# Issuing the load of the filter's rows from GpSimd's queue in a spectral convolution

## The chip, the cores and the metric

The kernel runs on one core of one Trainium2 chip. The metric is device time in microseconds of one execution; the time before is the median of three runs. One more execution was taken by the hardware profiler, and every duration below comes from that one. Engines are named as in the profile: PE is TensorE (PEld its weight loads), DVE is VectorE, ACT is ScalarE, POOL is GpSimd, SP is SyncE; SPq and POOLq are the queues in which an engine's sequencer takes its instructions, DMA issues among them.

## The reference

The input `x` is four images of 512 x 512 pixels with 16 channels, float32. There are two residual layers, each on a group-normalised input (8 groups). Layer 0 is a long convolution: a 16 x 16 matrix of transfer functions is made from 8 x 8 polynomial coefficients, `x` is transformed on a zero-padded 1024 x 1024 grid, each frequency is multiplied with the 16 x 16 matrix, and the result is transformed back and cut. Layer 1 is a 3 x 3 convolution with a normalisation, an arccos and two tanh factors.

```
X = jnp.fft.rfft2(x, s=(2 * l1, 2 * l2), axes=(-3, -2))
Y = jnp.einsum('...hwi,ijhw->...hwj', X, H_full)
y = jnp.fft.irfft2(Y, s=(2 * l1, 2 * l2), axes=(-3, -2))
```

## The kernel before

Four stages follow one another. `filter_phase` builds the filter's spectrum and leaves it in device memory as `g_d`. `forward_phase` transforms the normalised images along one axis and leaves them as `x_d`. `conv_phase` takes one row of the spectrum after another, does the transform along the other axis, the product and the way back, and stores `y_d`. `last_phase` finishes the inverse transform and does layer 1. The change is in `conv_phase` alone.

`conv_phase` works through 513 rows (`rows`, line 719; the first two are two halves of one row and take the `plane` branch). For each row there are these pieces:

- `load_x(n)` (line 743) brings the row of the images, 256 KB, into one of two buffers `x`.
- `load_g(n)` (line 731) brings the row of the filter, 128 partitions of 8 KB, 1024 KB in all, into one of two buffers `g`.
- `x_part(n, b)` (line 769) multiplies `x` with a DFT matrix on PE into `px`, which ACT and DVE copy to `xe`.
- `x_late(n)` (line 784) runs on POOL: it stores `xe` to `xf_d` (448 KB), makes a turned copy `xl` with four multiplications, a multiplication and an addition (lines 798 to 800), and stores `xl` to `xf_d` too (448 KB). Then `half_shift` copies two halves within the chip on ACT.
- `load_xe(n)` (line 812) reads `xf_d` back at shifted offsets, with two DMAs of 1536 KB each. These are the shifted copies. They read what both stores of `x_late(n)` wrote, so they wait until those have landed.
- `g_part(n, j)` (line 821) multiplies `g` with a DFT matrix on PE into `pg`, which is copied to `gh`. The last of them, j = 15, frees the buffer `g`.
- `mix(n, g)` (line 838) multiplies `gh` with `xe` on PE. It needs the shifted copies.
- `over_q` (line 858) and `over_g` (line 888) turn the product back on PE, DVE, ACT and POOL (`zd` and `z`, lines 882 and 884), and store `yo` to `y_d` from POOL (line 914, 256 KB).

`step(n)` (line 922) is a software pipeline: in it row n is mixed, row n + 1 has its filter transformed and its shifted copies loaded, row n + 2 has its images transformed, turned and stored, row n + 2 has its filter loaded, row n + 3 has its images loaded, and rows n - 1 and n - 2 are turned back. So `mix(n + 1)` comes two steps after `x_part(n + 1)`.

An automatic scheduler (Tile) sets the order of instructions within each engine's queue, from the data dependencies, the buffers and its own estimate of when each instruction can start; it also sets the waits. A queue is worked in order: an instruction that waits holds all behind it. In the trace the SP queue has, in each row, the order first half of the shifted copies, filter row, second half of the shifted copies, image row. The POOL queue has `xu`, store of `xe`, `xu`, `xl`, store of `xl`, store of `yo`, `zd`, `z`.

Of the kernel before, what the change touches and what calls it, by code (L numbers as in the profile page):

```python
# [46 lines left out]
P = 128  # L47
# [148 lines left out]
def dram(t, row, offset, *dims):  # L196

    pitch = t.shape[1]
    lead = [[pitch, t.shape[0]]] if row is None else []
    return bass.AP(tensor=t.tensor, offset=t.offset + (row or 0) * pitch + offset,  # L200
                   ap=lead + [list(d) for d in dims])
# [494 lines left out]
def conv_phase(tc, cst, g_d, x_d, y_d):  # L696
    nc = tc.nc
    with ExitStack() as ctx:
# [32 lines left out]
        def load_g(n):  # L731
            rc, r, plane = rows[n]
            g = io.tile([P, C, 8 * C], F32, name="g")
            t, w = g.rearrange("p j x -> p (j x)"), C * 8 * C
            if plane is None:
                nc.sync.dma_start(out=t, in_=dram(g_d[rc], r, 0, [w, P], [1, w]))
            else:
                for to, at in ((0, (0, 96)[plane]), (64, (64, 32)[plane])):
                    nc.sync.dma_start(out=t[to : to + 32], in_=dram(g_d[rc], r, at * w, [w, 32], [1, w]))
                    nc.gpsimd.memset(t[to + 32 : to + 64], 0.0)  # L740
            state["g", n] = g
# [180 lines left out]
        def step(n):  # L922
# [7 lines left out]
            if row(2):  # L930
                load_g(n + 2)
# [505 lines left out]
```

## Time and profile before

| what | value |
|---|---|
| median of 3 runs | 16687.61 us (16677.77 to 16700.49) |
| the profiled execution | 16676.9 us |
| its span | 16675.0 us |
| mean granted PE clock | 0.97 |
| first and last `g_part` matmul (about the length of `conv_phase`) | 4762.5 to 13817.4 us |
| busy PE / DVE / ACT / POOL over the span | 90% / 64% / 54% / 62% |
| device memory traffic over the span | 270 GB/s |
| DMA share, 6000 to 13700 us | 0.87 at 322 GB/s |

Busy time says how long an engine worked, not what it waited for; the ends of matmuls are modelled, and a busy PE is not a PE at its peak. A wait is read as "who waited, for whom, how long in total, how often, the longest". For a DMA the row of the issue shows only the issuing; its bytes move later, on 16 DMA engines that all queues share. The DMA share of a stretch is the mean busy share of those 16 engines; it can pass 1 slightly, since packets overlap.

### The profile page before, as it was taken

The numbers are of one execution on the slowest core, as the hardware profiler recorded it, in microseconds if no ns is written. First come the engines' busy times: TensorE is split into PE (matmuls) and PEld (weight loads), VectorE is DVE, ScalarE is ACT, GpSimd is POOL, SyncE is SP. The second block draws the span as 40 slices with busy tenths as digits, with TensorE's granted clock in tenths as the row PEclk, the third lists the DMA queues.
The fourth block names the chain that finished last, engine by engine and source line by source line (L and its number), as shares of the span: only waits on it lengthen the run. The fifth ranks groups of instructions, "written<-read, shape, count | busy, mean of one in ns | idle before, by whom it ended". The sixth has DMA issues, their size and how long they took to land. (4 is left out here: it accounts for less than half of the span.)

```text
span 16675.0 us, 545650 instructions
## 1 busy us (share of the span) xinstructions
PE 15084.4 (90%) x232588; PEld 11256.3 (68%) x232588; DVE 10610.7 (64%) x22299; ACT 9049.8 (54%) x18799; POOL 10372.0 (62%) x10669
## 2 busy tenths in 40 slices
PE   7999999998988898888888898888888888988888
PEld 5555555554557777777777777777777777867777
DVE  8999999993545555555555555555555552357877
ACT  5666666663345555555555555555555551027888
POOL 7777777772346666666666666666666660237766
PEclk7999999999999999999999999999999999989999
DMA  4888788878878888888888888888888886885531
GB/s 134 231 237 236 233 241 234 237 227 259 248 267 323 325 326 317 321 320 318 321 324 324 325 325 321 324 324 321 324 321 321 324 322 230 312 291 164 169 108 70
DMA packets 2914698, 4543.40 MB, mean 272 GB/s; under 512 B 126114, under 2 KB 2094460, under 8 KB 2801422
## 3 DMA queue, kind: packets, MB, share of 16 engines
q1 hardware_dynamic: 2703070, 3836.37, 67.4%
q0 software_dynamic: 172336, 605.00, 9.4%
q10 hardware_dynamic: 36864, 67.13, 1.2%
q8 instruction: 1833, 30.03, 0.7%
q14 instruction: 595, 4.87, 0.1%
HBM read 3030.71 MB, written 1477.31 MB: 270 GB/s over the span
## 5 line engine op out<-in xcount | busy, mean ns | idle before, releaser
L829 PE MATMUL pg<-c_dg,g 64*128 64x128 f32 x32832 | 2837.4, 290 | 357.0 <-ACT gh L729 186.6
L845 PE MATMUL pm<-xe,gh 128*32 128x64 f32 x131328 | 2386.6, 222 | 538.5 <-issue 286.2
L845 PEld LDWEIGHTS pm<-xe,gh 128*32 128x32 f32 x131328 | 2007.6, 110 | 1133.5 <-issue 933.1
L829 PEld LDWEIGHTS pg<-c_dg,g 64*128 64x128 f32 x32832 | 2286.2, 190 | 692.3 <-issue 260.3
L874 DVE TENSOR_TENSOR z<-zq,pz 128x256 f32<-128x256 f32 x2052 | 861.6, 420 | 2667.5 <-ACT zq L873 2597.6
L727 DVE COPY gh<-pg 128x512 f32<-128x512 f32 x2046 | 1409.9, 689 | 1242.8 <-PE pg L829 1237.6
L449 PE MATMUL pt<-ev_in,c_todd 128*128 128x512 f32 x4096 | 1928.0, 609 | 108.6 <-ACT u L337 83.4
L798 POOL TENSOR_TENSOR xu<-xe,c_late 128x256 f32<-128x256 f32 x2052 | 1394.3, 705 | 863.7 <-ACT xe L729 842.8
L506 DVE RECIPROCAL dn<-dn 128x256 f32<-128x256 f32 x1024 | 1718.1, 1718 | 0.0
L729 ACT COPY yf<-pm 128x512 f32<-128x512 f32 x2046 | 1211.0, 592 | 915.4 <-PE pm L845 901.4
L381 POOL TENSOR_TENSOR sp<-m,dn 128x512 f32<-128x512 f32 x1024 | 1302.6, 1273 | 611.8 <-DVE dn L506 527.1
L809 ACT COPY xe<-xl 64x1024 f32<-64x1024 f32 x513 | 538.7, 1050 | 1895.8 <-POOL xl L800 1895.8
L449 PEld LDWEIGHTS pt<-ev_in,c_todd 128*128 128x128 f32 x4096 | 728.6, 190 | 1022.1 <-issue 701.5
L729 ACT COPY gh<-pg 128x512 f32<-128x512 f32 x2058 | 1201.2, 584 | 378.9 <-PE pg L829 376.6
L866 PE MATMUL pz<-c_ident,yf 128*128 128x128 f32 x8208 | 1372.2, 290 | 29.9 <-issue 17.3
L397 PEld LDWEIGHTS pg<-c_dinv,sp 64*128 64x128 f32 x16384 | 1004.2, 196 | 466.2 <-ACT sp L386 211.4
L408 ACT COPY st<-pg 128x256 f32<-128x256 f32 x2048 | 617.6, 391 | 1281.9 <-PE pg L397 1281.9
L800 POOL TENSOR_TENSOR xl<-xl,xu 128x1024 f32<-128x1024 f32 x513 | 1209.7, 2358 | 40.2
L397 PE MATMUL pg<-c_dinv,sp 64*128 64x128 f32 x16384 | 1106.6, 287 | 72.4 <-ACT sp L386 48.3
L882 POOL TENSOR_TENSOR zd<-z 128x512 f32<-128x512 f32 x513 | 653.1, 1273 | 771.7 <-DVE z L874 771.7
L914 POOL DMA_DIRECT2D y_d<-yo x511 | 297.3, 582 | 1332.6 <-ACT yo L729 1306.8
L1280 PE MATMUL pc<-l_band,xn 128*128 128x160 f32 (+2 forms) x6144 | 1072.9, 333 | 52.2 <-DVE e_o L1335 51.9
(211 smaller groups left out, 30943.8 us busy)
## 6 DMA issues: line engine op xcount, KB each, us to landing
xe<-xf_d SPq DMA_DIRECT2D x1026, 1536.0 KB
g<-g_d SPq DMA_DIRECT2D x511, 1024.0 KB
g_d<-st SPq DMA_DIRECT2D x256, 1024.0 KB
ev_in<-g_d SPq DMA_DIRECT2D x1024, 256.0 KB
g_d<-ot SPq DMA_DIRECT2D x1024, 256.0 KB
xf_d<-xe POOLq DMA_DIRECT2D x513, 448.0 KB, 8.3
xf_d<-xl POOLq DMA_DIRECT2D x513, 448.0 KB, 5.5
x_d<-xo SPq DMA_DIRECT2D x128, 1024.0 KB
```

What stands on the lines that cost most here:

```text
L381: nc.gpsimd.tensor_mul(w["sp"], w["m"], bc(w["dn"], 2, [P, 2, 2, P]))
L397: nc.tensor.matmul(pg[u][:, n, k].rearrange("p a x -> p (a x)"), w["sp"][q, k, c, :], dinv[q, 2 * kp + k, c, :], start=(c == 0), stop=(c = ...
L449: nc.tensor.matmul(pt, todd[:, c, kc, hh * P : hh * P + P], ev[:, kc, c], start=(kc == 0), stop=(kc == 1),)
L506: nc.vector.reciprocal(w["dn"], w["dn"])
L727: nc.vector.tensor_copy(dst, src)
L729: nc.scalar.copy(dst, src)
L798: nc.gpsimd.tensor_mul(u[:, :, h, c], xe[:, :, h, 1 - c], bc(late[:, 1 + c], 2, [P, F, 2]))
L800: nc.gpsimd.tensor_add(xl.rearrange("p f h c k -> p (f h c k)"), xl.rearrange("p f h c k -> p (f h c k)"), u.rearrange("p f h c k -> p (f ...
L829: nc.tensor.matmul(pg[c][:, j % 4], g[half, j], dg[half], start=True, stop=True)
L845: nc.tensor.matmul(pm[32 * q : 32 * q + 32, g % 8], gh[:, f].rearrange("p c j -> p (c j)"), xe[:, :, f].rearrange("p t h c k -> p t (h c k ...
L866: nc.tensor.transpose(pz[:, t % 4].rearrange("p v q x -> p (v q x)"), y[:, at].rearrange("p g x -> p (g x)"), ident)
L1280: nc.tensor.matmul(pc[:, lo:hi, :].rearrange("p w j -> p (w j)"), xns[q][:, h * P + dh : h * P + dh + P], bands[dh][:, o : o + hi - lo, :] ...
```

## The change

The load of a whole filter row is issued by POOL and no longer by SP. The four half loads of the first two rows stay in SP's queue. Source, destination, buffers and size of the transfer are the same.

```
         def load_g(n):
             rc, r, plane = rows[n]
             g = io.tile([P, C, 8 * C], F32, name="g")
             t, w = g.rearrange("p j x -> p (j x)"), C * 8 * C
             if plane is None:
-                nc.sync.dma_start(out=t, in_=dram(g_d[rc], r, 0, [w, P], [1, w]))
+                nc.gpsimd.dma_start(out=t, in_=dram(g_d[rc], r, 0, [w, P], [1, w]))
             else:
```

More of the change, by code (lines that the diff above doesn't have):

```diff
@@ L735, in load_g @@
             if plane is None:
-                nc.sync.dma_start(out=t, in_=dram(g_d[rc], r, 0, [w, P], [1, w]))
+                nc.gpsimd.dma_start(out=t, in_=dram(g_d[rc], r, 0, [w, P], [1, w]))
             else:
```

## The prediction

> **What bounds the kernel now.** I read the page first for the stages, then the waits of PE and SP in the row loop, then the order of time of one row on SP and POOL, and then the DMA share microsecond by microsecond.
>
> The page, its PE row and the slices of DMA:
>
> ```profile
> span 16675.0 us, 545650 instructions
> PE 15084.4 (90%) x232588; PEld 11256.3 (68%) x232588; DVE 10610.7 (64%) x22299; ACT 9049.8 (54%) x18799; POOL 10372.0 (62%) x10669
> DMA  4888788878878888888888888888888886885531
> ```
>
> No engine is full, and neither is DMA. In the row loop, which lasts from about 4750 to 13850 us, PE waits for these (us in total, times, longest):
>
> ```profile
> PE pm L845 <- issue: 286.2, 305, 3.2
> PE pg L829 <- ACT gh L729: 186.6, 204, 3.9
> PE pg L829 <- issue: 167.3, 100, 3.4
> PE pm L845 <- DMA xe<-xf_d: 110.7, 75, 3.5
> ```
>
> The fourth line is what the change can reach: 110.7 us in which `mix` stood for the shifted copies, in 75 of some 511 rows, 1.5 us each. Four more rows of that answer name DVE instructions that `mix` doesn't read (z L878 14.8, zq L875 12.2, z L874 10.1, pz L876 8.0; 45.1 us together); part of these may be the same wait under another name. SP's own waits in the same stretch:
>
> ```profile
> SPq L815 <- DMA xf_d<-xl: 6612.7, 512, 15.5
> ...
> SPq L736 <- PE pg L829: 113.5, 140, 11.4
> SPq L736 <- PE pz L866: 92.1, 104, 1.8
> ```
>
> SP stands 12.9 us in every row (6612.7 / 512) until the store of `xl` has landed. Only then does it issue the shifted copies, and the filter row comes behind the first of them. One row in order of time, SP and then POOL:
>
> ```profile
> 9025.13 0.37 SPq L815 DMA_DIRECT2D xe<-xf_d  x1
> 9025.62 0.41 SPq L736 DMA_DIRECT2D g<-g_d  x1
> 9026.07 0.43 SPq L815 DMA_DIRECT2D xe<-xf_d  x1
> ```
>
> ```profile
> 9020.86 0.58 POOL L791 DMA_DIRECT2D xf_d<-xl  x1 [0.29 <-POOL xl L800]
> 9023.82 0.58 POOL L914 DMA_DIRECT2D y_d<-yo  x1 [2.37 <-ACT yo L729]
> 9026.38 1.27 POOL L882 TENSOR_TENSOR zd<-z 128x512 f32<-128x512 f32 x1 [1.98 <-DVE z L874]
> 9027.73 1.27 POOL L884 TENSOR_TENSOR z<-z 128x512 f32<-128x512 f32 x1
> 9030.07 1.36 POOL L798 TENSOR_TENSOR xu<-xe,c_late 128x256 f32<-128x256 f32 x2 [1.07 <-ACT xe L729]
> ```
>
> And the same stretch in windows of 1 us (after the colon: length, busy of PE, PEld, DVE, ACT, POOL, clock, DMA share, GB/s):
>
> ```profile
> 9023.00:9024.00 1.00, 1.00 (x58) 0.91 (x48) 0.87 (x3) 0.75 (x3) 0.18 (x1) 1.00 0.72 240
> 9024.00:9025.00 1.00, 1.00 (x18) 0.88 (x15) 0.79 (x4) 0.49 (x2) 0.40 (x1) 1.00 0.17 70
> 9025.00:9026.00 1.00, 1.00 (x26) 0.71 (x27) 0.65 (x2) 0.83 (x2) 0.00 (x0) 1.00 0.63 238
> 9026.00:9027.00 1.00, 1.00 (x64) 0.91 (x54) 0.90 (x4) 0.10 (x1) 0.62 (x1) 1.00 0.72 111
> 9027.00:9028.00 1.00, 1.00 (x15) 0.88 (x14) 0.72 (x3) 0.53 (x2) 0.92 (x2) 1.00 0.98 365
> ```
>
> There is a hole in the DMA traffic of each row, while SP waits for `xl` and until the first bytes of the shifted copies move; before and after it the engines are full. The trace also has a record of each DMA packet. Averaged over 380 rows and placed by the issue of the first shifted load (time 0), the DMA share is 0.97 at +14, 0.73 at +15, then 0.55, 0.26, 0.16 for the three microseconds about the next issue, 0.79 and then full from +2 on. That is a hole of some 2.5 us a row.
>
> The loop behind it runs over two rows. From the start of a `mix` to `x_part` is 2.6 us (9008.46 to 11.07), from there to the issue of the `xl` store 9.8 us (to 9020.86), to its landing and the first shifted load 5.7 us (landing 5.5 in the median), from there to the last packet of the shifted copies 15.1 us (median of the packet records), and about 1.2 us until the landing is known (estimate: the fastest `xl` store lands 3.4 us after issue, of which 2.2 are 1.13 to its first packet and 1.1 of packets). Sum 34.4 us for two steps, 17.2 us a row. PE alone needs 16.9: a third of the rows take 16.89 to 16.96 us from `x_part` to `x_part`, and these don't wait for the shifted copies. The mean row takes 17.6 us (513 rows from 4758.1 to 13785.4). So the loop and PE are nearly level; PE gains on the loop in quiet rows, catches up, and waits. The rest over 16.9 is PE's own ("issue" 1.0 us a row, and reduced clock now and then) and isn't touched.
>
> **What the skill says.** "DMA: Bandwidth & Descriptors", section Issuing engines are not separate DMA queues: DMAs from any engine run on the same 16 DMA engines, and another issuer saves only issue time. The packet records agree as to rate: 4 KB packets take 159 ns in POOL's queue and in SP's. The same page, section Queues, rings and completion order: each DMA engine takes turns between queues, a packet at a time, and within a queue works in ring order. The trace agrees in part: at +10 both queues move (0.34 and 0.66 of the engines). So `g` in SP's ring stands between the two shifted loads; in POOL's it stands behind the stores of `xl` and `yo` and shares with SP's. The same page, Specifications: first byte after about 1 us from GpSimd, about 0.6 us from Sync. Here it is 1.13 us after a `yo` store and 1.03 us after a shifted load, but 4.4 us after the `xe` store, which has POOL's multiplications behind it.
>
> **The change, part by part.**
>
> *SP loses one issue a row*, 0.44 us in the median, and with it the wait for `g_part` ahead of it: (113.5 + 92.1 + 15.4 + 7.5) / 511 = 0.45 us a row. The second shifted load is issued up to 0.9 us earlier. Worth nothing by itself: its bytes stand behind the first one's, 24 packets of 159 ns = 3.8 us on each engine.
>
> *POOL gains one issue a row.* The nearest row is the `yo` store, also 128 partitions, 0.58 us; 511 x 0.58 = 298 us of POOL time. It must wait for the last `g_part` of row n, which ends 2.1 us before the first shifted load in the median (4.0 us before `x_part` starts). I place it where it becomes free: after the `yo` store, ahead of `zd`. POOL idles there (1.98 us in the row shown; 771.7 us over 509 rows), because `zd` needs results that PE makes after that `g_part`. So it costs 0; behind it stand `zd`, `z` and the whole of `x_late`, so without the cover it would be 0.58 us a row in the two-row loop, 0.29 a step, up to 150 us; below zero it cannot go.
>
> *The bytes move earlier.* `g` is 8 packets of 309 ns on each engine, 2.5 us. Issued at -2.0 with 1.13 us to the first packet it starts at -0.9, behind what is left of the stores; the shifted load's packets start at +1.03. Of those 1.9 us about 1.5 are free (share 0.16 to 0.26 taken). So about 1.5 us of the 2.5 are moved in the hole, and the rest shares with the first shifted load. The last packet of the shifted copies comes 1.5 us earlier, at 13.6 instead of 15.1. Bounds: 0 (`g` starts no earlier than now) and 2.5 (all in the hole, in rows where PE is ahead and `g_part` ends at -3 or before). The loop becomes (34.4 - 1.5) / 2 = 16.45 us, below PE's 16.9: what is late next is PE itself.
>
> *The sum.* Of 110.7 us, with 1.5 us of relief against waits of 1.5 us mean and a loop with slack, I take 85% away: 94. Of the 45.1 us under other names a third: 15. Against this some 20 us for PE's waits named "issue": if they are instruction fetches over the same DMA engines, then filling the hole takes from them what the emptier end of the row gives back; bounded by 50 us either way, a tenth of their 521 us. Net -89 on the profiled execution, 16676.9 to about 16588; the median stood 11 us above that, so 16600. In POOL's queue `g` is needed 15.5 us after its present issue (shortest tenth about 14), and it lands within 11 now, earlier then: no new wait on PE.
>
> **The rivals.**
>
> *Hidden anyway (0.17), about 16680.* The shifted copies wait for bytes, and the bytes are the same. If POOL reaches the load only when the first shifted load goes out too, both queues share and the last packet stays at 15.1. For: in a quarter of the rows `g_part` ends less than 1 us before that issue. Against: those are the rows in which PE is behind and doesn't wait.
>
> *Slower (0.14), about 16950.* The load stands behind `zd` and `z` in POOL's queue, issued at +3.9 in the row shown. Then its packets, starting at +5 to +8, lie in one ring ahead of the `xe` store (issued at +5.3), and the `xl` store behind both lands up to 2.5 us later. The loop grows to (34.4 + 2.5) / 2 = 18.45; against today's 17.6 that is at most 0.8 us, over 511 rows 430 us, and half of it where they overlap less, with 260 as its value. It decides as soon as `xl` lands over 0.5 us later than now. For: the queue of POOL is in order, and the scheduler may put the load late. Against: `g_part` ends before the last `over_q`, which `zd` needs, so the load is ready first.
>
> *Larger gain (0.07), about 16480.* The `xl` store, its contention gone too, lands 1 us earlier, and PE's "issue" waits shrink by a fifth with the shorter backlog. Speaks against it: the total of bytes a row is unchanged.
>
> The forecast has 0.62.
>
> **How the numbers follow.** This kernel's measurement can tell about 0.2% from no change, 33 us, so 16654 and 16721 are the limits. Faster: 0.62 + 0.07 = 0.69. Same: 0.17. Slower: 0.14. The likeliest's own range is 16540 to 16650 (the hold of the 110.7 us and the bounds of the issue term). The range runs from 16510, which leaves out most of the larger gain, to 16730, which takes in no change and the edge of the slower case.
>
> **What would show it.** Right: in POOL's order the load of `g` between the `yo` store and `zd`, issued before the first shifted load; the DMA share in the hole risen; PE's wait for the shifted copies under 30 us; PE's "issue" near 521 us; rows of 16.9 us in more than half of the row loop. Wrong: the load behind `z`; the landing of `xl` above its 5.5 us or of `xe` above 8.3; `zd` or `xu` waiting for POOL's issue; or a new wait of `g_part` for `g`.

## The result

The changed kernel takes 16789.28 us in the median of four runs (16773.5 to 16796.37). On the same chip the kernel before took 16682.69 (16665.89 to 16700.49). The ratio is 1.0062 with the interval [1.0045, 1.0080]: slower by about 107 us. The prediction said 16600 and faster.

**The profile after.** The head of the page, its PE row, its DMA slices, and the table of DMA queues (packets, MB, share of 16 engines' time):

```profile
span 16771.7 us, 545635 instructions
PE 15112.5 (90%) x232588; PEld 11245.3 (67%) x232588; DVE 10630.4 (63%) x22299; ACT 9107.3 (54%) x18799; POOL 10634.8 (63%) x11180
...
DMA  4788887888878888888888888888888886885531
...
q1 hardware_dynamic: 2629486, 3300.51, 58.1%
q0 software_dynamic: 245920, 1140.85, 18.9%
q10 hardware_dynamic: 36864, 67.13, 1.2%
q8 instruction: 1833, 30.03, 0.7%
```

The span is 96.7 us longer, and PE works 28 us of that (15112 against 15084); the rest it waits. All of it lies in the row loop: from the first `x_part` to the last it was 9027.3 us before and is 9124.8 now. The row loop before and after (length; busy of PE, PEld, DVE, ACT, POOL; clock, DMA share, GB/s):

```profile
4758.10:13785.40 9027.30, 8062.22 (x183716) 6454.86 (x183717) 4900.70 (x13245) 4759.39 (x8679) 5763.23 (x5624) 0.98 0.87 322
4754.80:13879.60 9124.80, 8087.89 (x183717) 6440.42 (x183718) 4922.02 (x13245) 4817.45 (x8679) 6029.63 (x6134) 0.98 0.87 319
```

PE worked 26 us longer in the loop and stood 72 us longer (965 before, 1037 after). The filter's bytes went from q1 to q0. The last line of the queue table becomes important below: a queue named "instruction", 0.7% of the engines, the same 1833 packets in both kernels.

PE's waits in the row loop (total us, times, longest), the answer to the four lines shown of before:

```profile
PE pm L845 <- issue: 630.0, 559, 4.3
PE pg L829 <- issue: 170.0, 127, 3.7
PE pm L845 <- ACT zq L873: 80.8, 224, 0.7
PE pg L829 <- ACT gh L729: 57.8, 71, 4.1
...
PE pm L845 <- DMA xe<-xf_d: 0.2, 1, 0.2
```

The wait that the change was to take away went from 110.7 to 0.2 us, and the wait for ACT's copies of `gh` from 186.6 to 57.8. In their place stands "issue", the profile's name for time in which an engine waits for nothing that it shows: `mix` 630.0 instead of 286.2, `g_part` 170.0 instead of 167.3, and with the three smaller groups 896 us instead of 521. All of PE's waits in the loop, whatever they are named, add up to 980 us before and 1047 after: of the 375 us that "issue" gained, 307 are taken from other waits.

One row on POOL and then on SP:

```profile
9025.53 0.58 POOL L914 DMA_DIRECT2D y_d<-yo  x1 [3.34 <-ACT yo L729]
9027.06 0.54 POOL L736 DMA_DIRECT2D g<-g_d  x1 [0.94 <-PE pg L829]
9028.31 1.27 POOL L882 TENSOR_TENSOR zd<-z 128x512 f32<-128x512 f32 x1 [0.71 <-DVE z L874]
9029.67 1.26 POOL L884 TENSOR_TENSOR z<-z 128x512 f32<-128x512 f32 x1
```

```profile
9026.30 1.79 SPq L815 DMA_DIRECT2D xe<-xf_d  x2
9032.19 0.33 SPq L748 DMA_DIRECT2D x<-x_d  x1
```

The load of `g` stands where the prediction put it, between the store of `yo` and `zd`, in time in which POOL idled. In this row it goes out 0.8 us behind the first shifted load; in two rows of three it goes out ahead of it. The landing of the `xl` store (min, median, max), before and then after:

```profile
DMA to landing us min/median/max: 3.4/5.5/8.7
```

```profile
DMA to landing us min/median/max: 3.4/4.2/10.0
```

It lands 1.3 us earlier, so the shifted loads start earlier too. The filter, the `xl` store and the shifted copies all came earlier, and PE lost more than that won.

**What "issue" is here.** The waits called "issue" sit at fixed places. I counted all that PE's sequencer takes, in its order: matmuls, weight loads and the instructions on semaphores between them. Of the matmuls' "issue" gaps over 0.4 us in the row loop, 377 of 378 before and 650 of 651 after come at the same place of each group of 256 instructions. The trace has 2 x 232588 matmuls and weight loads and 4230 others on PE, which make 1833.6 such groups; the instruction queue has 1833 packets of 30.03 MB / 1833 = 16.4 KB, or 64 bytes for each of 256 instructions. With packets and blocks both counted from the start, the packet that had ended last before PE went on was in every such stall the one of that block's number. So PE stands for the refill of its own instructions. The Trainium skill, "Runtime: NRT & Kernel Launch", section Instruction fetch mechanics, describes this: blocks of 16 KiB, 256 instructions, which the sequencer fetches with a DMA queue of its own while it works off the block before. The counts agree. It also says that the cost is "mostly hidden"; here some 590 us before and 980 after are not hidden, and the measurement decides.

(These two figures take in gaps of the weight loads too and so lie above "issue", which counts the matmuls' alone.) One such stall, PE's weight loads in order of time (in brackets the idle time before):

```profile
9140.43 0.97 PEld L829 LDWEIGHTS pg<-c_dg,g 64*128 64x128 f32 x16
9144.11 0.42 PEld L866 LDWEIGHTS pz<-c_ident,yf 128*128 128x128 f32 x4 [2.71 <-issue]
```

The block in use had begun at 9137.15. By the packet records the next block's packet was under way only from 9141.61 to 9142.58, and PE went on at 9144.11, 1.5 us after its end. Over all stalls that last step is 1.4 us (1.23 to 1.6 in nine of ten), and the packet takes about 1.0 us, in both kernels. What differs is the delay from the start of one block to the start of the packet for the next. I sorted the blocks by what the DMA engines moved in the 1.5 us after a block began. Before, the delay is 1.1 us in the median where the DMA share was under 0.2; 3.7 where the share was over 0.8 and most of it shifted copies or filter rows; but 2.2 where most of it was POOL's stores. After, loads gave 4.1 and stores 1.9. So it is the loads that the late refills stand beside, not any full DMA engine. A block lasts 3.6 to 8 us on PE without its stall. With a delay of 4, the sum 4 + 1.0 + 1.4 = 6.4 us is longer than two blocks of three last.

The same place in windows of 1 us (after the colon: length, busy of PE, PEld, DVE, ACT, POOL, clock, DMA share, GB/s):

```profile
9142.00:9143.00 1.00, 0.00 (x0) 0.00 (x0) 0.00 (x0) 0.00 (x0) 1.00 (x1) 1.00 1.01 406
9143.00:9144.00 1.00, 0.08 (x1) 0.00 (x0) 0.00 (x0) 0.96 (x1) 0.58 (x2) 1.00 1.01 412
9144.00:9145.00 1.00, 1.00 (x9) 0.65 (x10) 0.69 (x1) 0.98 (x3) 0.00 (x0) 1.00 1.04 369
9145.00:9146.00 1.00, 1.00 (x10) 0.67 (x8) 0.48 (x2) 0.45 (x2) 0.00 (x0) 0.71 0.89 291
9146.00:9147.00 1.00, 1.00 (x8) 0.53 (x6) 0.93 (x4) 0.00 (x0) 0.00 (x0) 0.50 0.62 227
9147.00:9148.00 1.00, 1.00 (x20) 0.34 (x19) 0.07 (x1) 0.23 (x1) 0.00 (x0) 0.50 0.05 12
```

DMA share is 1.0 while PE stands, and 1.3 us after it goes on the clock falls to 0.5. That is the second part of the price. The clock records change in steps of 3.413 us, the window that "TensorE: Matmul & The Clock Gate", section What's actually happening, states, with the half rate it gives. That section asks for an idle window. In these traces less is enough: a window of the row loop at full clock with 2.0 us or more of PE idle was followed by half clock every time (47 of 47 before, 63 of 63 after), one with 1.5 to 2.0 about every second time (38 of 68, 35 of 82), one with less hardly ever. PE's "issue" spells of over 2 us went from 55 to 96; with those of other names, above all the wait for the shifted copies, from 78 to 100. So the half clock grew less than the refills: it lasted 356 us of the row loop before and 400 after. At half speed 44 us more cost about 22 (an estimate: half of them), which is nearly all of the 26 us that PE worked longer. About three quarters of the loss is standing, one quarter slow work.

The loss lies in few rows. I took the 485 rows in the middle of the loop. Where no half clock begins nothing changed: 17.22 us before (405 rows) and 17.20 after (395), the wait for the shifted copies exchanged for refills. The rows in which one begins went from 80 of 19.77 us to 90 of 20.62. Over 17.2 us this is 80 x 2.57 = 206 us before and 90 x 3.42 = 308 after, and that difference of 102 us is about the lost time. These rows are slow by both parts: they also hold the longest stalls. Over the whole loop, in the rows that any half clock touches, PE stood 2.7 us a row before and 3.7 after, and worked 16.8 and 17.2.

### The profile page after: what moved, and what is told of

It is laid out like the page before. It is cut to its first block, busy times and chain, and to the rows that moved or that the text cites. A ratio compares the mean times of both kernels' runs of the same rounds, so it can differ in the third digit from the quotient of the medians.

```text
span 16771.7 us, 545635 instructions
## 1 busy us (share of the span) xinstructions
PE 15112.5 (90%) x232588; PEld 11245.3 (67%) x232588; DVE 10630.4 (63%) x22299; ACT 9107.3 (54%) x18799; POOL 10634.8 (63%) x11180
## 3 DMA queue, kind: packets, MB, share of 16 engines
q8 instruction: 1833, 30.03, 0.7%
## 5 line engine op out<-in xcount | busy, mean ns | idle before, releaser
L845 PE MATMUL pm<-xe,gh 128*32 128x64 f32 x131328 | 2454.1, 222 | 718.8 <-issue 630.0
L829 PE MATMUL pg<-c_dg,g 64*128 64x128 f32 x32832 | 2782.2, 291 | 230.0 <-issue 170.0
L829 PEld LDWEIGHTS pg<-c_dg,g 64*128 64x128 f32 x32832 | 2247.1, 190 | 568.6 <-issue 271.6
L903 PE MATMUL py<-z,c_ig 128*64 128x256 f32 x6156 | 1078.4, 412 | 38.0 <-issue 35.8
```

Source lines behind the costliest of these rows:

```text
L829: nc.tensor.matmul(pg[c][:, j % 4], g[half, j], dg[half], start=True, stop=True)
L845: nc.tensor.matmul(pm[32 * q : 32 * q + 32, g % 8], gh[:, f].rearrange("p c j -> p (c j)"), xe[:, :, f].rearrange("p t h c k -> p t (h c k ...
L903: nc.tensor.matmul(py[64 * half : 64 * half + 64, odd], ig[:, s0, c2], zs.rearrange("p (t h) j -> p h t j", h=2), start=(c2 == 0), stop=(c ...
```

## The experiments

Two theories stood at first. **A**: GpSimd's queue is at fault; its ring with the stores and the filter load delays the refills, or its instructions hold something. **B**: the queue is indifferent; the early place is at fault. The pause in the DMA traffic that I wanted to fill was where the refills for the end of the row ran. The expectations also name a theory C, an even exchange: what PE no longer waits for the shifted copies it waits for its instructions.

### The filter load early, in SP's queue and in ACT's

`g_first_sp` keeps it in SP's queue and puts it ahead of both shifted loads. `InOrder`, here and below, fixes the order of the instructions that the named engine gets inside its `with` blocks:

```
-        flip = [0]
+        flip, loads = [0], InOrder(tc, nc.sync)
...
-            if row(2):
-                load_g(n + 2)
-            if row(1):
-                load_xe(n + 1)
+            with loads:
+                if row(2): load_g(n + 2)
+                if row(1):
+                    load_xe(n + 1)
```

> The filter row stays in SP's queue but is put ahead of both shifted loads, so it starts as early as in the changed kernel, in SP's own ring. Theory A (a second busy ring: PE's instruction fetches wait longer because each DMA engine takes turns among more queues): PE's waits named issue in the row loop stay near 520 us as before, the wait for the shifted copies falls under 20, time 16580 to 16650. Theory B (the hole: fetches were served in the hole of the DMA traffic, and whatever fills it costs): issue waits 800 to 950 us, time 16760 to 16820, as in the changed kernel. Theory C (exchange: what PE no longer waits for the shifted copies it waits for its instructions): issue waits 620 to 700, time within 0.2% of before.

`g_act_queue` issues it from ACT:

```
-                nc.sync.dma_start(out=t, in_=dram(g_d[rc], r, 0, [w, P], [1, w]))
+                nc.scalar.dma_start(out=t, in_=dram(g_d[rc], r, 0, [w, P], [1, w]))
```

> The filter row is issued from ACT's queue, in a ring of its own that hardware fills, at the place behind the last zq copy of a row. It goes out about when the first shifted load does or up to 1 us earlier. Theory A: issue waits 800 to 950 us as in the changed kernel, 16740 to 16820. Theory B: the hole is filled in part, issue waits 600 to 800, 16690 to 16780. If only a ring filled by GpSimd does harm, it is like before: issue near 520, 16600 to 16690.

`g_first_sp` took 16864.1 us against 16720.4, ratio 1.0087 [1.0073, 1.0101], and `g_act_queue` 16747.49, ratio 1.0015 [1.0008, 1.0022] (its profiled execution was slower, span 16767.1). PE's waits of `g_first_sp` and then of `g_act_queue`:

```profile
PE pm L845 <- issue: 629.2, 544, 4.5
PE pg L829 <- issue: 187.3, 120, 3.5
```

```profile
PE pm L845 <- issue: 679.0, 600, 4.3
PE pg L829 <- issue: 192.4, 139, 3.9
```

Both look like the changed kernel, with 944 and 956 us of "issue", and in `g_first_sp` POOL has nothing of the filter. Theory A falls by `g_first_sp`, for which it had named about 520 us, and so does C, with 620 to 700; the time is above what B had named. `g_act_queue` alone wouldn't have told: its "issue" is just above A's 800 to 950 and well above B's 600 to 800. That ACT's version is less slow than `g_first_sp` with as much "issue" is in part its other waits: PE waits 71 us for ACT in it and 159 in `g_first_sp`, and stands 1022 us in the row loop against 1103. Why ACT is waited for less I didn't isolate.

### The filter load last, in SP's queue

`g_last_sp` calls `load_xe(n + 1)` ahead of `load_g(n + 2)`:

> The filter row stays in SP's queue behind both shifted loads; the hole stays open, and the shifted copies land 2.5 us earlier. Theory A: issue waits near 520 us, wait for the shifted copies gone, 16570 to 16650. Theory B: the same as A, since the hole is kept: 16570 to 16650. Theory C: issue waits rise by about the 110 us that are saved, 16660 to 16720. If the filter row then comes too late for its transform, PE waits for it at line 829 and the time is above 16720.

16714.85 us against 16720.39, ratio 0.9997 [0.9989, 1.0005]. PE's waits:

```profile
PE pm L845 <- issue: 351.6, 363, 4.8
...
PE pg L829 <- issue: 149.1, 104, 3.8
PE pg L829 <- DMA g<-g_d: 85.2, 90, 3.0
```

The wait for the shifted copies is gone as in the changed kernel, and the refills are not worse by much. But `g_part` now waits for the filter, 85.2 us, and the time stays. "Issue" came to 566 us. The price of a late landing is moved, not removed; A and B had both named 16570 to 16650, which missed; the time lies in what C named, but with less "issue" and by another wait.

### Fewer bytes, and smaller pieces

`g_eighth` keeps the order of before and loads an eighth of the filter row (128 KB); every `g_part` multiplies the same two slices, so the filter's values are not those of the reference:

```
-            g = io.tile([P, C, 8 * C], F32, name="g")
+            g = io.tile([P, 2, 8 * C], F32, name="g")
...
-                nc.sync.dma_start(out=t, in_=dram(g_d[rc], r, 0, [w, P], [1, w]))
+                nc.sync.dma_start(out=t, in_=dram(g_d[rc], r, 0, [w, P], [1, w // 8]))
...
-                nc.tensor.matmul(pg[c][:, j % 4], g[half, j], dg[half], start=True, stop=True)
+                nc.tensor.matmul(pg[c][:, j % 4], g[half, j % 2], dg[half], start=True, stop=True)
```

> Only an eighth of the filter row is loaded (128 KB instead of 1024), in SP's queue at the old place, and the transform reads that eighth again and again; this part of the computation is changed. All theories have PE waiting for instructions because the DMA engines are full: 0.9 MB of 5.4 a row are gone, so issue waits fall from 520 to under 250 us, the wait for the shifted copies to under 20, and the time to 16200 to 16400. If the issue waits stay near 520, they don't hang on the DMA traffic.

16634.69 us, ratio 0.9954 [0.9937, 0.9971]: 86 us faster, far from what I expected. DMA share in the row loop fell from 0.87 to 0.77, and still:

```profile
PE pm L845 <- issue: 482.9, 486, 3.8
PE pg L829 <- issue: 160.5, 115, 3.1
```

With all five groups 693 us, more than the 521 of before. Fewer bytes let the `xl` store land in 3.4 us, so the shifted loads start earlier in PE's row. This was the first sign that the place of the burst counts, and not its size alone.

`xe_2k_pieces` and `xe_1k_pieces` cut the pieces of the shifted loads from 4 KB to 2 and 1 KB, with two or four DMAs each; the bytes are the same. If a refill had to wait for a number of packets ahead of it, smaller packets would shorten its wait.

```
-            for t in (1, 5):
+            for t, s in [(t, s) for t in (1, 5) for s in range(2)]:
...
-                                ap=[[XF, P], [C * XF, 3], [1, XF]]),
+                                ap=[[XF, P], [C * XF, 3], [1, XF // 2]]),
```

> The kernel before, but each shifted load is issued as two DMAs with pieces of 2 KB per partition instead of one with pieces of 4 KB; the bytes, and the place of the filter row, stay. The theory now: PE stands still because its next 256 instructions (one packet of 16 KB, of the instruction queue) start up to 4 us late behind the data packets that each DMA engine has already taken in, and a stand of 2 us in a window of 3.4 us halves PE's clock for the next window. If the backlog is a number of packets, pieces of half the size halve the delay (from about 4 us to 2 to 2.5 in the burst), issue waits fall from 520 to under 300 us and the time to 16450 to 16600. If the backlog is a number of bytes or of microseconds, the delay and the issue waits stay, and the time is within 0.3% of before (16690 to 16770).

> The same with four DMAs of 1 KB pieces for each shifted load. If the backlog is a number of packets: delay in the burst about 1.2 to 1.5 us, issue waits under 200 us, but smaller packets move fewer bytes a second (4 KB take 159 ns, 2 KB 84), so that the shifted copies land later: 16450 to 16750. If not: issue waits near 520 and 16750 to 16950 for the lower rate.

17155.03 us, ratio 1.0258 [1.0244, 1.0272], and 17428.88 us, ratio 1.0426 [1.0412, 1.0440]. A 4 KB packet takes 159 ns and a 2 KB packet 84, but the refill's delay in the burst stayed at 3.9 and 3.8 us. So it isn't a count of packets. Both times are above all that I had named, since the copies land later. In `xe_1k_pieces` PE's two waits turn over:

```profile
PE pm L845 <- DMA xe<-xf_d: 381.8, 346, 2.6
...
PE pm L845 <- issue: 211.0, 242, 3.0
```

It looks as if refills came while PE waited for data, so that the two waits stand in for each other. But in `xe_2k_pieces` both rose, the wait for the copies from 111 to 235 us and "issue" from 521 to 698. These runs also issue two and four times as many DMAs, which isn't separated from the size of the pieces.

### The filter load on POOL, but later

`g_pool_late` is the changed kernel with the load held behind `zd` and `z` in POOL's queue, the place of my slower rival. `g_between` holds it between the two. Both use `InOrder(tc, nc.gpsimd)`, and `load_g` in `step` then serves the first four rows alone; of `g_between`:

```
-                nc.gpsimd.tensor_sub(d, z[:, :, 4:6], z[:, :, 6:8][:, :, ::-1])
+                with loads: nc.gpsimd.tensor_sub(d, z[:, :, 4:6], z[:, :, 6:8][:, :, ::-1]); n + 4 < n_rows and load_g(n + 4)
...
-                nc.gpsimd.tensor_add(z[:, :, 4:6], z[:, :, 4:6], z[:, :, 6:8][:, :, ::-1])
+                with loads: nc.gpsimd.tensor_add(z[:, :, 4:6], z[:, :, 4:6], z[:, :, 6:8][:, :, ::-1])
```

> The filter row is issued by POOL as in the changed kernel, but one place later, behind zd and z, some 3 to 4 us after the first shifted load, so that the hole in the DMA traffic at the end of a row stays open. If the hole is what matters: fetches at the end of a row (13 to 17 us after x_part) start 1.9 to 2.6 us after the block began, as before, and not 4 us; issue waits 500 to 620 us instead of 900; the wait for the shifted copies under 30; time 16620 to 16720, so at or just under before. If POOL's queue or ring is what matters: issue waits 800 or more, 16770 to 16850. My rival of the prediction (the stores behind it in the ring land late): the xl store lands above 5.5 us in the median and the shifted copies are waited for, 16850 to 17000.

> The changed kernel with the filter load held in POOL's queue between zd and z, some 2 us after the first shifted load's issue instead of ahead of it. A dose between the changed kernel and g_pool_late. If the early start of the burst is the cause: PE's issue waits 550 to 700, refill delay 13 to 17 us after the start of x_part 2.2 to 3.5 us, wait for the shifted copies 0 to 100, time 16670 to 16770, below the changed kernel. If any filter load in POOL's queue ahead of z costs the same: issue waits near 900, time 16780 to 16820.

`g_pool_late`: 16716.69 us against 16672.63, ratio 1.0025 [1.0014, 1.0036]. `g_between`: 16653.79 against 16686.61, ratio 0.9982 [0.9972, 0.9992]. The POOL order of `g_between`, and its waits:

```profile
9026.11 1.29 POOL L882 TENSOR_TENSOR zd<-z 128x512 f32<-128x512 f32 x1 [1.27 <-DVE z L874]
9027.36 0.55 POOL L736 DMA_DIRECT2D g<-g_d  x1
9027.92 1.27 POOL L884 TENSOR_TENSOR z<-z 128x512 f32<-128x512 f32 x1
```

```profile
PE pm L845 <- issue: 317.8, 304, 3.3
PE pg L829 <- ACT gh L729: 195.8, 216, 4.2
PE pg L829 <- issue: 143.1, 94, 3.4
PE pm L845 <- DMA xe<-xf_d: 101.8, 83, 2.8
```

The load is in POOL's queue as in the changed kernel; it is issued about 2.4 us later in PE's row, and the profile is that of before again, both waits included ("issue" 531 us). That is no halfway dose, which I had expected, but the whole way back. This is the plainest witness for B. It fell below the kernel before by 0.18%, at the edge of what can be told apart, and is the fastest complete version here. In `g_pool_late` "issue" came to 599 us, as B had it, but the copies were still waited for, 101.7 us and not under 30, and it is a little slower than before. `xl` lands at 5.4 us, as before: what my slower rival feared didn't happen even in its own place.

### The same two kernels once more

> The kernel before, unchanged, profiled once more, to see how far PE's waits scatter between two profiles of one kernel. If the 593 us of stalls at refill places are a property of the kernel's order: issue waits of PE in the row loop 480 to 570, wait for the shifted copies 80 to 140, mean refill delay 13 to 17 us after the start of x_part below 2.6 us. If they are chance: issue waits anywhere from 450 to 900.

> The changed kernel, unchanged, profiled once more. If its stalls come from where its burst of loads starts in PE's row: issue waits 820 to 980, wait for the shifted copies under 10, refill delay 13 to 17 us after the start of x_part above 3.7 us. If chance: anywhere from 450 to 900, and then the difference of the two kernels isn't explained by it.

16670.98 and 16782.02 us. "Issue" came to 569 us (521 in the first profile) and 919 (896); the wait for the shifted copies to 97.8 and 1.3. Of `after_again`:

```profile
PE pm L845 <- issue: 648.6, 575, 4.0
PE pg L829 <- issue: 170.3, 129, 4.8
```

Two profiles of one kernel differ by up to 50 us here, the kernels by 330 to 400. It is a property of their order. The second pair divides the loss much as the first: in the row loop PE stood 85 us longer and worked 51 longer.

### Filling the pause with other bytes

`fill_hole` is the kernel before with 512 KB of constants stored from POOL in each row, right behind the `yo` store, to nowhere that is read; `fill_late` has the same stores behind `z`; `loads` is `InOrder(tc, nc.gpsimd)`.

```
-                nc.gpsimd.dma_start(out=dram(y_d[rc], r, 0, [4 * P, P], [1, 4 * P]), in_=yo)
+                with loads: nc.gpsimd.dma_start(out=dram(y_d[rc], r, 0, [4 * P, P], [1, 4 * P]), in_=yo); [nc.gpsimd.dma_start(out=fill_d[n % 4][v], in_=(c_dfs, c_ig)[v]) for v in range(2)]
```

> The kernel before with nothing moved, and 512 KB a row of added stores of constants to unused memory, issued by POOL right behind the yo store, so at the end of the row, in the hole. If the filled hole is what makes PE's fetches late: at 13 to 17 us after x_part the fetch delay rises from 1.9 to 2.4 us to about 3 or more, issue waits from 520 to 650 to 800, time 0.4 to 1.0% above before. If only the sum of bytes matters, it is as far from before as the twin run with the same stores behind z.

> The twin: the same 512 KB of added stores, issued by POOL behind z, in the middle of the burst. The hole stays, but the shifted copies land up to 1.3 us later. If the hole is what matters: fetch delay at 13 to 17 us after x_part stays at 1.9 to 2.4 us, issue waits stay within 80 us of 520; the wait for the shifted copies rises from 110 to 200 to 500 us, time 0.5 to 2.5% above before by that wait. If only the sum of bytes matters: issue waits like those of the twin run.

16852.61 us, ratio 1.0108 [1.0094, 1.0122], and 17229.48, ratio 1.0336 [1.0322, 1.0350]. The refill's delay 13 to 17 us after `x_part` in `fill_hole` was 2.5 to 2.8 us, under the 3 that I expected, and "issue" rose to 609 only, although the pause was filled: from 13 to 17 us after `x_part` the DMA share, microsecond by microsecond, is 0.68, 0.97, 1.08 and 0.73 in the undisturbed rows, against 0.58, 0.84, 0.31 and 0.50 before and 0.20, 0.83, 0.82 and 1.00 in the changed kernel. Bytes in the pause alone don't make the changed kernel. The added bytes are stores, and beside stores the refills were less late in the other traces too; a run with added loads, which would settle it, was not made. The time rose more than the changed kernel's, by PE's work as much as by its waits. In `fill_late` "issue" fell to 344 us, lower than I had named, and the exchange is the clearest:

```profile
PE pm L845 <- DMA xe<-xf_d: 468.1, 196, 4.5
...
PE pm L845 <- issue: 160.9, 196, 2.9
```

### The filter early, the shifted loads not

In all three early versions (the changed kernel, `g_first_sp`, `g_act_queue`) the shifted loads start earlier as well. `shifted_held` takes that away: in the changed kernel SP issues four transfers of 64 bytes between the landing of `xl` and the first shifted load. `before_held` does the same to the kernel before; `loads` is `InOrder(tc, nc.sync)`.

```
-            src = xf_d[n % 4]
+            src, hold = xf_d[n % 4], xlp.tile([1, 16 * 4], F32, name="hold", bufs=2)
+            with loads: [nc.sync.dma_start(out=hold[:, 16 * m : 16 * m + 16], in_=src[P : P + 1, :16]) for m in range(4)]
             for t in (1, 5):
-                nc.sync.dma_start(
+                with loads: nc.sync.dma_start(
```

> The changed kernel with four small transfers of 64 bytes on SyncE between the landing of the xl store and the first shifted load; they delay the issue of the shifted loads by about 1.3 us (four issues of about 0.33 us, the nearest row being the load of own), and the filter load on GpSimd stays as early as it is. If what hurts is that the shifted loads start earlier in PE's row: PE's issue waits fall to 480 to 650, refill delay 13 to 15 us after the start of x_part below 2.8 us, time 16640 to 16740, no slower than before. If what hurts is the filter's own packets in the pause: issue waits stay above 820, refill delay there above 3.7, time 16780 or more.

> The kernel before with the same four small transfers ahead of its first shifted load, as the control for what they cost. The shifted copies land about 1.3 us later than PE meets them now: wait for the shifted copies 250 to 600 instead of 111, issue waits 300 to 480, time 16800 to 17000. If PE isn't bound by the start of the shifted loads on this side: both within 10% of the kernel before, time 16670 to 16720.

`shifted_held`: 16740.46 us against 16689.65, ratio 1.0030 [1.0019, 1.0041]. The four issues took 1.12 us and some 1.3 to the shifted load. PE's waits:

```profile
PE pm L845 <- issue: 455.4, 484, 4.6
PE pg L829 <- issue: 171.2, 111, 3.5
...
PE pm L845 <- DMA xe<-xf_d: 13.8, 7, 3.0
```

"Issue" is 715 us, midway between 521 and 896: neither of my two cases. Both the filter's early packets and the earlier start of the shifted loads cost, by this run about half each. `g_eighth`, an early start with hardly any filter, lies at 693 from the other side. The share of each is an estimate: the held loads start at -1.3 us, later than in the kernel before (-2.1). `before_held` took 17176.14 us, ratio 1.0296 [1.0281, 1.0312], dearer than I expected: the wait for the shifted copies rose to 495.1 us, and half clock began in 179 of its rows before 13600 us, where it was about 80 in the kernel before. So the kernel before stands between two slopes, and the later side is far steeper.

### All of them by the start of the burst

Times are medians, relative to the start of `x_part` in the same row; the delay is the mean of refills whose block begins 13 to 15 us after `x_part` started, which is 2 to 4 us ahead of the next one. Stalls are the sum at the refill places in the row loop, weight loads included. Half clock is counted in the rows in which it begins.

| kernel | issue of `g` | first shifted load | refill delay | stalls, us | rows with half clock, mean us | ratio |
|---|---|---|---|---|---|---|
| before | -1.6 | -2.1 | 1.85 | 593 | 80, 19.77 | 1 |
| `before_again` | -1.9 | -2.3 | 1.91 | 661 | 78, 19.76 | |
| `g_between` | -1.1 | -1.6 | 1.85 | 582 | 68, 19.48 | 0.9982 |
| `g_last_sp` | -1.4 | -2.5 | 2.12 | 676 | 91, 19.94 | 0.9997 |
| `g_pool_late` | +0.3 | -2.1 | 1.97 | 655 | 94, 19.64 | 1.0025 |
| `shifted_held` | -3.6 | -1.3 | 4.05 | 826 | 68, 20.69 | 1.0030 |
| `g_eighth` (an eighth of the filter) | -3.1 | -3.6 | 3.93 | 773 | 72, 20.37 | 0.9954 |
| changed | -3.5 | -3.2 | 4.24 | 978 | 90, 20.62 | 1.0062 |
| `after_again` | -3.4 | -3.2 | 4.27 | 993 | 92, 20.69 | |
| `g_first_sp` | -3.7 | -3.0 | 4.27 | 1002 | 93, 20.97 | 1.0087 |
| `g_act_queue` | -2.9 | -3.2 | 4.13 | 1037 | 93, 20.60 | 1.0015 |

Where both loads start at -2.5 or later the stalls are 582 to 676 us. Where both start at -2.9 or earlier with the whole filter they are 978 to 1037. Where only one does, or the filter is an eighth, they lie between. The queue that issues the filter makes no such difference. The time follows less strictly than the stalls, since other waits count too: PE stands 1103 us in the row loop of `g_first_sp`, 1037 in the changed kernel, 1022 in `g_act_queue`, 965 in the kernel before and 910 in `g_eighth`.

## Why the prediction was wrong

- **SP's issue, worth nothing.** Right. SP's wait ahead of the image load grew from 1146.4 to 2302.6 us, and nobody waited for it.
- **POOL's issue, hidden ahead of `zd`.** Right: 0.54 us each; POOL's wait for `zd`'s input shrank from 771.7 to 366.3 us, and 206.5 us of what it gave up is now its wait for `g_part` ahead of `g`.
- **The bytes move earlier.** Right in PE's row, wrong in how. Against the first shifted load `g` came 0.5 us ahead in the median row, not 2.0, because that load itself moved ahead by 1.1 us in PE's row as `xl` landed 1.3 us earlier. So `g` mostly shared with the shifted loads: their last packet came 14.9 us after the first issue, 15.1 before, and not at 13.6. Where `g` is as far ahead as I had it (2.3 us in `shifted_held`), the last packet does come at 13.9, and the copies are waited for 13.8 us in all. In the changed kernel what spared PE the wait was the earlier landing, which I had only in the rival with the larger gain, and by `shifted_held` that is also about half of the rise in "issue".
- **85% of the wait for the shifted copies goes.** Right in size, and more: all of it went. As the point above says, the reason was mostly another than the one I gave.
- **"Against this some 20 us for PE's waits named "issue""; "filling the hole takes from them what the emptier end of the row gives back; bounded by 50 us either way, a tenth of their 521 us".** This step failed. I guessed what these waits were, and then bounded them without looking where they stood. They rose by 375 us, to 896, where I had 20 in the sum. The emptier end of the row does give back: blocks that begin 6 to 11 us after `x_part` are refilled after 2.3 and 2.1 us instead of 3.6 and 2.9. But those blocks last 5 to 7 us and had only 20 us of stalls in all, 11 and 9, to give. The pause lay where blocks of 5 to 6 us, those beginning 13 to 17 us after `x_part`, were refilled in 1.9 to 2.4 us; these lost their cover and went from 73 to 198 us of stalls. The next row's blocks at 3.5 to 6, already deep in the burst, went from 202 to 430, in part because more blocks begin there (395 instead of 284). A tenth of their sum was no bound, since the sum could nearly double. The other waits shrank by 307 us in the meantime, more than I had counted on, and the loop still lost: 72 us of standing and 26 of slower work.
- **PE's floor of 16.9 us is "what is late next".** Right as a floor, wrong as what follows: 41% of the rows are below 16.96 us (38% before), not more than half. The exchange left the undisturbed rows equal and made the slow ones slower, through longer stalls and the half clock behind them, which I had called "now and then" and "isn't touched".
- **The rivals.** Hidden anyway (16680) has the wrong waits; the slower one (16950) had the right sign for a reason that didn't occur, with `g` not behind `z` and `xl` not late. None named the refill as what makes it slower. My list of what would show me wrong held one thing that told: "issue" near 521.

Open is why a refill waits about 4 us in a burst of loads, whatever the packets' size, and about 2 beside stores. That PE waits for its refills is shown by their place and the packet times, and that the place of the loads makes them late by `g_between` against the changed kernel; what holds them back isn't shown.

## What to carry to other kernels

A pause in the DMA traffic may be in use by something that no wait names: in a kernel with many small instructions, look whether "issue" gaps repeat every so many instructions of an engine, and place them in time before an early transfer is put into the pause. Compare a wait that is removed with all those that stood behind it: here 459 us of other waits fell to 151, and the one that I had taken for nearly fixed rose by 375. A place for a transfer is best tried on both sides (here -3.5, -1.1 and +0.3 us gave 1.0062, 0.9982 and 1.0025).

## What was new about the hardware

- PE's instruction blocks, 16 KB for 256 instructions, wait with the data on the DMA engines: about 1 us to their packet in a pause, about 4 beside loads, about 2 beside stores, then 1.0 us of packet and 1.4 until PE goes on.
- That delay didn't follow the size of the data packets: about 4 us with packets of 159 ns, 3.9 and 3.8 with halves and quarters of them.
- PE's clock was halved after every full-clock window of 3.413 us that held 2.0 us or more of idle time, though not wholly idle (110 of 110 in the two row loops).
- Reading the same bytes in 2 KB pieces in place of 4 KB, with twice the DMAs, made this kernel 2.6% slower, in 1 KB pieces with four times the DMAs 4.3%.
